# The last half sequence of a recurrence and its experts, taken as two parts of 256 tokens

## The chip, the cores and the metric

The kernel runs on one core of a Trainium2 chip. The core has five engines that work side by side, each with its own queue of instructions in a fixed order: TensorE (PE) for matmuls, VectorE (DVE), ScalarE (ACT), GpSimd (POOL), and SyncE (SP), which here issues most of the DMA transfers. They wait for each other through semaphores. The metric is device time of one launch in microseconds. The profile is one launch recorded by the hardware profiler.

## The reference: what is computed

Four layers, each with an attention-like part and a feed-forward part, act on 4 sequences of 1024 tokens with 128 features. The change touches the last layer only. It has a selective state-space recurrence, and then eight experts with gates:

```
x   = rms_norm(resid) * norm_w
xs  = silu(causal_conv4(x @ in_w.T) + conv_b)            # 256 channels
d   = softplus(xs @ wd1.T @ wd2.T + wd2_b)
h_t = exp(d_t * A) * h_{t-1} + (d_t * xs_t) * B_t        # 16 states a channel, over time
y   = (h . C + xs * W_D) * silu(x @ skip_w.T) @ out_w.T
x   = layernorm(resid + (resid + y))
gate = probs * keep          # softmax router, most probable experts up to a sum of 0.8
x   = layernorm(x + sum_e gate_e * (relu(x @ W1_e + b1_e) @ W2_e + b2_e))
```

All eight experts are computed for every token, and the gates weight their results. The recurrence runs along time, so a later piece of a sequence needs the last state of the piece before it (16 states for each of 256 channels), and the convolution needs the last three tokens.

## The kernel before, in words

The last layer takes the tokens in eight half sequences of 512. Each goes through these steps, written as Python generators that yield between small groups of instructions:

- l3_prepare: normalisation, input projection (matmul pxe), convolution on DVE (xc), silu (xs), the projections pdb, and softplus on ACT and DVE (dl, ud). The rows of B and C go out to DRAM by an SP DMA (rows).
- l3_scan: for each of 16 states n, two SP DMAs broadcast row n of B and of C over the partitions (bn, cn, four buffers each). POOL multiplies db = ud * bn, ACT computes da = exp(dl * A) into PSUM, DVE runs the scan (L1828), POOL multiplies hc = db * cn. From the second sequence on every second hc is added to the one before by an accumulating DMA that POOL issues (L1843), and PE sums what is left over the states with an identity matmul (pys).
- l3_sum and l3_finish: the skip gate (psk), the output projection (po), layer normalisation, transposition of the result (pt), and the router (prl, then about 15 short DVE instructions) that ends in the gates gt.
- l3_ffn_head: transposes the gates (pgt), ACT copies them (gT), a matmul adds the experts' second biases (pb), and DVE starts the accumulator h_acc.
- l3_ffn: for each expert four matmuls ph of 512 columns, relu on ACT (hh), sixteen matmuls py, and four DVE instructions that add gate times result to h_acc. At the end layer normalisation and the output DMA (L183). An expert's weights, 512 KB, come by an SP DMA into one of three wh buffers (l3_weights), asked for two experts ahead.

The function l3 lays these over each other. While the scan of one half runs, each of its 16 states also advances the finish of the half before, the preparation of the half after, and three or four steps of the experts (work), which belong to the half two back. A half is given to the experts a few states after its router (the age in todo). After the last scan the finish of the last half runs beside the experts of the last but one, then the experts of the last half follow. Once everything is handed over ("all"), the next change from one half's experts to another's also closes the PSUM banks of the scan and opens eight banks for the experts.

The generators only set the order in which instructions are written down. The framework then orders them on each engine by its own estimate of when each becomes ready, and each engine runs its list strictly in that order. So an instruction that waits holds up everything behind it on its engine: a pys that waits for hc holds up the experts' matmuls, and a bn DMA that waits for a buffer holds up the wh DMA behind it on SP.

Of the kernel before, what the change touches and what calls it, by code (L numbers as in the profile page):

```python
# [10 lines left out]
F32 = mybir.dt.float32  # L11
# [7 lines left out]
P = 128  # L19
# [39 lines left out]
class Net:  # L59
# [1513 lines left out]
    def l3(self, moe, fp):  # L1573
# [5 lines left out]
        halves = [dict(b=b, h=h) for b in range(B) for h in range(2)]  # L1579
        for i, u in enumerate(halves):  # L1580
            u["prev"] = halves[i - 1] if u["h"] else None
        halves[0] = dict(self.c3["first"], **{k: halves[0][k] for k in ("prev",)})
        for i, u in enumerate(halves[1:], 1):
            u["prev"] = halves[i - 1] if u["h"] else None
        work = self.l3_experts(fp)
        end = iter(())
        for i, u in enumerate(halves):
            nxt = iter(())
            if i + 1 < len(halves):
                if halves[i + 1]["h"] == 0:  # L1590
                    while "done" not in self.m2["st"][halves[i + 1]["b"]]:
                        next(moe)
                nxt = self.l3_prepare(halves[i + 1])
# [54 lines left out]
    def l3_weights(self, i, wp):  # L1648
        if i < 2 * B * NE:
# [18 lines left out]
    def l3_early(self, pool):  # L1668
# [19 lines left out]
        u = dict(b=0, h=0, at=at, ff=self.bank("pj"))  # L1688
# [3 lines left out]
    def l3_prepare(self, u):  # L1692

        nc, c3, b, h = self.nc, self.c3, u["b"], u["h"]
        at, ff, dp = u.get("at", self.l3_at), u.get("ff", self.bank("ff")), c3["dp"]
        wdb = c3["we"][:, :, 0:ND]

        sq = at("sq3", [P, 4, D])
        ms = self.sm.tile([P, 4], F32, name="ms3")
        for k in range(4):  # L1700
            nc.scalar.activation(
                sq[:, k, :], self.xN[b][:, 4 * h + k, :], AF.Square, accum_out=ms[:, k : k + 1]
            )
# [3 lines left out]
        for k in range(4):  # L1707
            nc.scalar.activation(
                sq[:, k, :], self.xN[b][:, 4 * h + k, :], AF.Copy, scale=ms[:, k : k + 1]
            )  # L1710
        yield
        pt = ff([P, 4, P], "pt")
        for k in range(4):
            self.tr(pt[:, k, :], sq[:, k, :])
        xnT = at("xnT", [P, 512])
# [6 lines left out]
        tail = at("tail", [P, 2, K1]) if h == 0 else u["prev"]["tail"]  # L1722
        u["tail"] = tail
        xs = at("xs3", [P, 2, 512])
        for ec in range(2):
            p = ff([P, 512], "pxe")
            self.mm(p, c3["wskip"][:, 1, ec * P : (ec + 1) * P], xnT)
            xc = at("xc", [P, 512])
# [3 lines left out]
            o = K1 if h else 0  # L1732
            nc.vector.tensor_scalar(xc[:, o:], p[:, o:], w[K1], bias, ALU.mult, ALU.add)
            if h:
# [3 lines left out]
            for d in range(1, KCONV):  # L1738
                nc.vector.scalar_tensor_tensor(
                    xc[:, d:], p[:, 0 : 512 - d], w[K1 - d], xc[:, d:], ALU.mult, ALU.add  # L1740
                )
            if h == 0:
                nc.vector.tensor_scalar(
                    tail[:, ec, :], p[:, 512 - K1 :], w[0], bias, ALU.mult, ALU.add
                )
                for d in range(K1 - 1, 0, -1):
                    nc.vector.scalar_tensor_tensor(
                        tail[:, ec, 0:d], p[:, 512 - d :], w[K1 - d], tail[:, ec, 0:d],
# [8 lines left out]
        db = at("db1", [ND, 512])  # L1757
        rows = dp.tile([2 * NST, 512], F32, name="rows")
        p = ff([ND, 512], "pdb")
# [6 lines left out]
        dl, ud = at("dl", [P, 2, 512]), at("ud", [P, 2, 512])  # L1766
        for g in ((0,), (1,)) if "at" in u else ((0, 1),):
            us, v = at("sp_u", [P, len(g), 512]), at("sp_w", [P, len(g), 512])
            p2 = []
            for k, ec in enumerate(g):  # L1770
                p2.append(ff([P, 512], f"pd{ec}"))
# [21 lines left out]
    def l3_scan(self, u):  # L1793


        nc, c3, b, h = self.nc, self.c3, u["b"], u["h"]
        sp, wp, aneg = c3["sp"], c3["wp"], c3["aneg"]
        wout = c3["we"][:, :, ND:]
        xnT, xs, dl, ud, rows = (u[k] for k in ("xnT", "xs", "dl", "ud", "rows"))
        carry = wp.tile([P, 2, NST], F32, name="carry") if h == 0 else u["prev"]["carry"]  # L1800
# [4 lines left out]
        def add(n, hc):  # L1805
            if not py:
                py.extend(self.psb(f"y{ec}", [P, 512], f"pys{ec}") for ec in range(2))
# [5 lines left out]
        for n in range(NST):  # L1813
            bc = []
            for i, nm in enumerate(("bn", "cn")):
                t = wp.tile([P, 1, 512], F32, name=nm, bufs=4)
                r = i * NST + n
                nc.sync.dma_start(
                    out=t[:, 0, :], in_=rows[r : r + 1, :].to_broadcast([P, 512])
                )  # L1820
                bc.append(t.to_broadcast([P, 2, 512]))
            db = wp.tile([P, 2, 512], F32, name="db", bufs=4)
            nc.gpsimd.tensor_mul(db, ud, bc[0])  # L1823
            for ec in range(2):
                j = ec * NST + n
                da = self.psb("da", [P, 512], "da")
# [5 lines left out]
                    carry[:, ec, n : n + 1] if h else 0.0,  # L1832
# [3 lines left out]
            if h == 0:  # L1836
                nc.scalar.copy(carry[:, :, n : n + 1], db[:, :, 511:512])
            hc = wp.tile([P, 2, 512], F32, name="hc", bufs=4)
# [25 lines left out]
    def l3_finish(self, u):  # L1864


        nc, c3, b, h = self.nc, self.c3, u["b"], u["h"]
# [4 lines left out]
        for ec in range(2):  # L1872
            p = ff([P, 512], "psk")
            self.mm(p, c3["wskip"][:, 0, ec * P : (ec + 1) * P], u["xnT"])

            t = sp.tile([P, 512], F32, name="th")
# [6 lines left out]
        po = ff([P, 4, D], "po")  # L1883
        for k in range(4):
# [9 lines left out]
        r = sp.tile([P, 4, D], F32, name="ss_r", tag="s2")  # L1894
        nc.vector.scalar_tensor_tensor(
            r, self.xN[b][:, 4 * h : 4 * h + 4, :], 2.0, po, ALU.mult, ALU.add
        )
        yield
        yield from self.norm_parts(wp, r, b, 4 * h, 4, ps=ff, act=True, slow=True)
        yield  # L1900
        n = NC // 2
        pr, g, rank, pj, cum = self.router(sp, b, c3["wr"], c3["br"], ps=ff, c0=4 * h, n=n)
# [12 lines left out]
    def l3_ffn_head(self, u, head, wp):  # L1915

        nc, c3, h = self.nc, self.c3, u["h"]
        ff = lambda s, n: self.psb("ff", s, n)
        acc = wp.tile([P, 4, D], F32, name="h_acc")
        head.append(acc)  # L1920
        pg = ff([NE, 4, P], "pgt")
        for c in range(4):
            self.tr(pg[:, c, :], u["gt"][:, c, :])
        gT = wp.tile([NE, 4, P], F32, name="gT", bufs=1)
        nc.scalar.copy(gT, pg)
        yield
        pb = ff([P, 4, D], "pb2")
        for c in range(4):
            self.mm(pb[:, c, :], gT[:, c, :], c3["b2"])
        nc.vector.tensor_add(acc, pb, self.xN[u["b"]][:, 4 * h : 4 * h + 4, :])  # L1930
# [247 lines left out]
```

## Time and profile before

| What | Value |
|---|---|
| Median of 3 runs | 2389.36 us (2387.49 to 2404.25) |
| The profiled execution | 2414.07 us, span 2412.3 us |
| Mean granted TensorE clock | 0.917 |
| Busy: PE, DVE, ACT, POOL | 2068.1, 1420.2, 1287.5, 863.0 us |
| First and last scan instruction of the layer on DVE | 1415.0, 2253.7 us |
| Experts, first and last ph | 1629.3, 2396.1 us |
| hc and db on POOL, 128 x 1024 elements | 2528 and 2638 ns each |
| Scan on DVE, 128 x 512, with carry | 1268 ns each |
| da on ACT, 128 x 512 | 689 ns each |

A row of instructions in the profile names the line, the engine, the operation, the result and the operands with their shapes, and how many there were. A matmul in 32-bit floats appears as two instructions. An idle time in brackets is what the engine waited before the instruction, with the engine or transfer that released it. All matmuls and transposes are issued from helper functions (L127, L131), so they are told apart by the names of their results: ph, py, pys and so on. Tiles keep their names in both kernels.

### The profile page before, as it was taken

What the parts mean: (1) busy time and instruction counts of PE and PEld (TensorE: products, weight loads), DVE (VectorE), ACT (ScalarE), POOL (GpSimd) and SP (SyncE); (2) the same over time, 40 slices, a digit from 0 to 9 for tenths busy, and PEclk for the clock granted to TensorE, in tenths of its full rate; (3) what the DMA queues carried; (4) which work ended last, traced back from release to release, by engine and by line L of the source; (5) the groups of instructions that cost most, each with busy time, mean ns of one, the idle gap of its engine ahead of it and who ended that gap; (6) DMA issues with size and microseconds to landing.
All of it is one profiled execution on the core that took longest, in us unless ns stands there. A gap on an engine that the chain in (4) does not pass through costs nothing.

```text
span 2412.3 us, 34775 instructions
## 1 busy us (share of the span) xinstructions
PE 2068.1 (86%) x12170; PEld 1454.9 (60%) x12170; DVE 1420.2 (59%) x3949; ACT 1287.5 (53%) x2679; POOL 863.0 (36%) x557
## 2 busy tenths in 40 slices
PE   6767979979899999999979965778797989899888
PEld 3455655544577787787767753346564656565566
DVE  6457733433455655655555676777777777687421
ACT  6543433332455555555556555565757766767443
POOL 5001220000000011001020148888877879589400
PEclk9657989989999999999999987789998989999899
DMA  3000110022000010021222155456764657476411
GB/s 101 0 18 20 32 31 9 9 86 71 1 1 1 1 34 21 11 81 43 65 64 82 35 181 176 140 176 178 193 198 135 181 154 207 139 205 176 114 57 49
DMA packets 138512, 209.84 MB, mean 87 GB/s; under 512 B 18597, under 2 KB 75936, under 8 KB 138080
## 3 DMA queue, kind: packets, MB, share of 16 engines
q1 hardware_dynamic: 126048, 172.82, 23.2%
q0 software_dynamic: 12288, 34.79, 6.9%
q8 instruction: 96, 1.57, 0.3%
q14 instruction: 80, 0.66, 0.1%
HBM read 159.24 MB, written 23.16 MB: 76 GB/s over the span
## 4 chain that ended last, share of the span: by engine, by line
PE 60%; DVE 18%; ACT 10%; issue 7%; DMA 2%; POOL 1%; another core or an unknown queue 1%; SPq 0%; ACTq 0%; POOLq 0%; DVEq 0%
PE ph L127 12%; PE py L127 8%; PE po L1118 4%; PE pqk L127 4%; PE po L127 4%; PE pt L131 4%; PE pa_m L127 3%; DVE db L1828 3%; PE pys L127 3%; PE po L1134 3%; PE kp_mo L127 3%; PE pv L127 2%; PE pr L127 2%; DVE a L1105 1%; PE kp_mo L131 1%
## 5 line engine op out<-in xcount | busy, mean ns | idle before, releaser
L1839 POOL TENSOR_TENSOR hc<-db,cn 128x1024 f32<-128x1024 f32 x128 | 317.1, 2528 | 88.8 <-PE pys L127 41.8
L1823 POOL TENSOR_TENSOR db<-ud,bn 128x1024 f32<-128x1024 f32 x112 | 287.1, 2638 | 29.3 <-DVE pmv L159 23.2
L127 PEld LDWEIGHTS py<-wh,hh 128*128 128x128 f32 x2048 | 253.7, 197 | 70.5 <-issue 40.9
L127 PE MATMUL ph<-xT,wh 128*128 128x512 f32 x512 | 265.3, 637 | 33.5 <-DVE h_acc L1967 13.4
L127 PE MATMUL py<-wh,hh 128*128 128x128 f32 x2048 | 259.8, 281 | 14.6 <-ACT hh L1951 9.5
L1951 ACT ACTIVATE hh<-ph,sb_cols 128x512 f32<-128x512 f32 x256 | 171.8, 682 | 158.6 <-PE ph L127 127.2
L1151 DVE SCALAR_TENSOR_TENSOR num<-po,sb_c_trig,nsin 128x130 f32<-128x130 f32 x256 | 89.2, 348 | 268.5 <-ACT nsin L1150 251.2
L1827 ACT ACTIVATE da<-dl,aneg 128x512 f32<-128x512 f32 x224 | 153.3, 689 | 66.7 <-DVE db L1828 63.2
L127 PE MATMUL pys<-hc,sb_c_ident 128*128 128x512 f32 x320 | 168.6, 655 | 15.6 <-POOL hc L1839 8.2
L1026 POOL MEMSET cv<- 128x16 f32 x32 | 4.1, 128 | 482.6 <-ACT cv L1043 365.5
L1828 DVE TENSOR_TENSOR_SCAN db<-da,carry,db 128x512 f32<-128x512 f32 x128 | 157.4, 1268 | 20.4 <-POOL db L1823 10.2
L127 PEld LDWEIGHTS ph<-xT,wh 128*128 128x128 f32 x512 | 93.9, 204 | 123.6 <-issue 56.5
L1150 ACT ACTIVATE nsin<-po,sb_c_trig 128x130 f32<-128x130 f32 x256 | 94.8, 370 | 131.7 <-PE po L1134 72.3
L1828 DVE TENSOR_TENSOR_SCAN db<-da,db 128x512 f32<-128x512 f32 x128 | 149.6, 1206 | 14.3 <-ACT da L1827 6.7
L127 PE MATMUL pqk<-xT,wE 128*128 128x256 f32 x512 | 138.9, 395 | 16.7 <-DVE cv L1036 13.7
L1967 DVE SCALAR_TENSOR_TENSOR h_acc<-py,gt,h_acc 128x128 f32<-128x128 f32 x256 | 72.1, 343 | 130.3 <-PE py L127 125.0
L1366 POOL DMA_INDIRECT xrows<-xN,di x64 | 62.4, 976 | 238.1 <-ACT kN L1070 230.6
L1118 PE MATMUL po<-cv,a 128*128 128x130 f32 x1024 | 138.7, 279 | 1.0 <-DVE num L1151 0.8
L1118 PEld LDWEIGHTS po<-cv,a 128*128 128x128 f32 x1024 | 126.8, 194 | 5.1 <-PE pqk L127 1.1
L1043 ACT ACTIVATE cv<-cv,sb_c_trig 128x520 f32<-128x520 f32 x128 | 86.5, 724 | 77.3 <-DVE cv L1036 68.2
L127 PEld LDWEIGHTS pys<-hc,sb_c_ident 128*128 128x128 f32 x320 | 63.3, 211 | 85.3 <-issue 60.4
L127 PEld LDWEIGHTS pqk<-xT,wE 128*128 128x128 f32 x512 | 88.5, 192 | 36.3 <-DVE cv L1036 18.1
(456 smaller groups left out, 4492.9 us busy)
## 6 DMA issues: line engine op xcount, KB each, us to landing
wx<-in_wF SPq DMA_DIRECT2D x92, 384.0 KB
bn<-rows SPq DMA_DIRECT2D x128, 256.0 KB
cn<-rows SPq DMA_DIRECT2D x128, 256.0 KB
wh<-in_wH SPq DMA_DIRECT2D x64, 512.0 KB
hc<-hc POOLq DMA_DIRECT2D x48, 512.0 KB
xrows<-zero SPq DMA_DIRECT2D x4, 1472.0 KB
xg<-xrows SPq DMA_DIRECT2D x20, 256.0 KB
yrows<-ys SPq DMA_DIRECT2D x20, 256.0 KB
```

Source lines behind the costliest of these rows:

```text
L127: return self.nc.tensor.matmul(out=out, lhsT=lhsT, rhs=rhs, start=start, stop=stop)
L131: self.nc.tensor.transpose(out, in_, self.ident[0:n, 0:n])
L1043: nc.scalar.activation(Q["v"][c][:, hs, i, :], v1[:, hs, :], AF.Copy, scale=c2["trig"][:, k, i : i + 1],)
L1118: self.nc.tensor.matmul(out=u["po"][:, i, c, :], lhsT=u["a"][:, i, c, :], rhs=Q["v"][c][:, 2 * hp + i, :, :].rearrange("p a d -> p (a d)") ...
L1134: self.nc.tensor.matmul(out=u["po"][:, i, c, :], lhsT=u["q"][h, s], rhs=Q["st"][h, hp, c, :], start=False, stop=True, skip_group_check=True,)
L1150: nc.scalar.activation(t, po[:, :, c, VW : 2 * VW], AF.Copy, scale=trig[:, k, 1:2])
L1151: nc.vector.scalar_tensor_tensor(num[:, c], po[:, :, c, 0:VW], trig[:, k, 0:1], t, ALU.mult, ALU.add)
L1823: nc.gpsimd.tensor_mul(db, ud, bc[0])
L1827: nc.scalar.activation(da, dl[:, ec, :], AF.Exp, scale=aneg[:, j : j + 1])
L1828: nc.vector.tensor_tensor_scan(db[:, ec, :], da, db[:, ec, :], carry[:, ec, n : n + 1] if h else 0.0, ALU.mult, ALU.add,)
L1839: nc.gpsimd.tensor_mul(hc, db, bc[1])
L1951: nc.scalar.activation(ht, ph, AF.Relu, bias=self.col("h_b1", i=e * NK + k))
```

## The change

The list of halves becomes a list of parts with a first chunk c0 and a length n in chunks of 128 tokens. The first seven parts are the half sequences as before (n = 4). The last half is replaced by two parts of n = 2. All shapes in the steps above follow n. The state (carry) and the last tokens for the convolution (tail) are kept whenever a part is not the last of its sequence, so they now pass from the first half of the last sequence to the first quarter part, and on to the second. The experts are run for nine parts instead of eight, so eight more loads of expert weights are issued. In an expert on 256 tokens the yield in the middle of py is left out.

```diff
-        halves = [dict(b=b, h=h) for b in range(B) for h in range(2)]
+        parts = [(b, h, 4) for b in range(B) for h in (0, 4)]
+        parts[-1:] = [(B - 1, 4, 2), (B - 1, 6, 2)]
+        halves = [dict(b=b, c0=c0, n=n, last=c0 + n == NC) for b, c0, n in parts]
         for i, u in enumerate(halves):
-            u["prev"] = halves[i - 1] if u["h"] else None
+            u["prev"] = halves[i - 1] if u["c0"] else None
...
     def l3_weights(self, i, wp):
-        if i < 2 * B * NE:
+        if i < self.c3["parts"] * NE:
...
     def l3_prepare(self, u):
+        L, first = n * P, c0 == 0
-        tail = at("tail", [P, 2, K1]) if h == 0 else u["prev"]["tail"]
-        u["tail"] = tail
-        xs = at("xs3", [P, 2, 512])
+        tail = None if first else u["prev"]["tail"]
+        u["tail"] = None if u["last"] else at("tail", [P, 2, K1])
+        xs = at("xs3", [P, 2, L])
...
     def l3_scan(self, u):
-                t = wp.tile([P, 1, 512], F32, name=nm, bufs=4)
+                t = wp.tile([P, 1, L], F32, name=nm, bufs=4)
...
-            db = wp.tile([P, 2, 512], F32, name="db", bufs=4)
+            db = wp.tile([P, 2, L], F32, name="db", bufs=4)
...
-                    carry[:, ec, n : n + 1] if h else 0.0,
+                    0.0 if first else carry[:, ec, n : n + 1],
...
-            if h == 0:
-                nc.scalar.copy(carry[:, :, n : n + 1], db[:, :, 511:512])
-            hc = wp.tile([P, 2, 512], F32, name="hc", bufs=4)
+            if not u["last"]:
+                nc.scalar.copy(carry[:, :, n : n + 1], db[:, :, L - 1 : L])
+            hc = wp.tile([P, 2, L], F32, name="hc", bufs=4)
...
     def l3_ffn(self, u, head, i0, wp, others):
-                ph = ff([P, 512], "ph")
+                ph = ff([P, n * P], "ph")
                 self.mm(ph, w[:, k * P : (k + 1) * P], x)
-                ht = wp.tile([P, 512], F32, name="hh", bufs=6)
+                ht = wp.tile([P, n * P], F32, name="hh", bufs=6)
...
-            py = ff([P, 4, D], "py")
-            for c in range(4):
+            py = ff([P, n, D], "py")
+            for c in range(n):
...
-                if c == 1:
+                if c == 1 and n > 2:
                     yield
```

## The prediction

> **What bounds the kernel now.** I number the half sequences 0 to 7. Half 7, the second half of the last sequence, is the one that becomes parts 7a and 7b. The views were read in this order: engine totals, then busy time by stage near the end, then TensorE's instructions at the stage boundaries, then who released each wait.
>
> Busy time by stage (columns: length, busy time of PE, its weight loads, DVE, ACT and POOL, then the granted clock and DMA):
>
> ```profile
> 2163.00:2184.00 21.00, 12.03 (x45) 6.43 (x43) 17.75 (x38) 13.44 (x19) 13.86 (x8) 0.84 0.64 166
> 2184.00:2256.00 72.00, 71.75 (x378) 48.98 (x376) 52.31 (x87) 47.95 (x76) 69.78 (x35) 1.00 0.66 182
> 2256.00:2275.00 19.00, 12.28 (x27) 6.17 (x28) 7.03 (x23) 4.44 (x9) 3.92 (x3) 0.64 0.39 88
> 2275.00:2344.00 69.00, 62.57 (x358) 46.15 (x356) 21.90 (x76) 29.22 (x44) 0.00 (x0) 0.97 0.20 61
> 2344.00:2404.00 60.00, 59.41 (x320) 41.99 (x320) 8.11 (x30) 22.88 (x36) 0.00 (x0) 0.95 0.17 49
> ```
>
> Row 2 is half 7's scan, with half 5's experts on PE beside it. PE is full at clock 1.00, and POOL nearly so. Rows 4 and 5 are the experts of halves 6 and 7 after the scan: PE again, and POOL has nothing left. Rows 1 and 3 are boundaries, where one scan ends and the next half's experts cannot start yet. PE loses time only there and at the hand-over at 2344.
>
> TensorE in order of time (start, length, what, then in brackets the idle before it and its releaser):
>
> ```profile
> 2250.21 3.82 PE L127 MATMUL py<-wh,hh 128*128 128x128 f32 x32
> 2253.86 1.88 PE L127 MATMUL pys<-hc,sb_c_ident 128*128 128x512 f32 x4
> 2261.48 1.02 PE L131 MATMUL pgt<-sb_c_ident,gt 128*8 128x128 f32 x4 [5.74 <-DVE gt L1910]
> 2263.73 2.07 PE L127 MATMUL pb<-sb_h_b,gT 8*128 8x128 f32 x8 [1.24 <-ACT gT L1925]
> 2265.74 5.49 PE L127 MATMUL ph<-xT,wh 128*128 128x512 f32 x6
> ...
> 2336.50 4.11 PE L127 MATMUL py<-wh,hh 128*128 128x128 f32 x32
> 2344.28 6.53 PE L127 MATMUL ph<-xT,wh 128*128 128x512 f32 x8 [3.67 <-DVE ln_nm L168]
> ...
> 2358.09 3.60 PE L127 MATMUL ph<-xT,wh 128*128 128x512 f32 x8
> 2361.53 3.73 PE L127 MATMUL py<-wh,hh 128*128 128x128 f32 x32
> ```
>
> At 2261 PE has waited 5.74 us for the router's gates (gt), then 1.24 us for their transpose's copy, and then runs at half clock: six ph take 5.49 us where six take 2.74 elsewhere. At 2344 it waits for the previous half's normalisation. The last two lines give the unit of work: an expert of 512 tokens is 3.44 us of ph and 3.57 us of py (start to start), 7.0 us.
>
> **The change part by part.**
>
> PE work: +0. The ph of 256 tokens stream half the columns. Matmuls of 512 columns start 0.43 us apart, those of 128 columns 0.11 us apart, so the time goes with the columns and 0.215 us is my estimate for 256. Twice as many at half length give 1.7 + 1.8 = 3.5 us per 256-token expert. The py, pys, pxe and psk keep their total columns. So the 221 us from 2183 to the last matmul still hold some 194 us of PE work: 24 experts of 512 tokens' worth (168) plus 26 of sums, projections and router. Splitting pulls nothing off PE. It lets half 6's experts and 7a's start inside the scan, but PE was not idle in the scan before. What can move is the time lost at boundaries, so I price those.
>
> New boundary, 7a to 7b. The nearest row is 2256:2275. From the first router instruction on DVE (2250.39) to gt (2261.43) took 11.0 us there. In the changed program's instruction order DVE also has the softplus chain of 7b in that stretch: ten instructions on 256 elements, 0.40 us each by the router's 128x256 rows, 4.0 us. It no longer has two scans there (2.45 us). So 12.6 us. Between router and gates PE has one expert's py (3.57) and the two pd (0.86). Idle 8.2, plus 1.2 for the copy. Then the half clock: pgt, pb and ph lost 0.4 + 0.9 + 2.75 = 4.1 us at 2261. The Trainium skill (TensorE: Matmul & The Clock Gate, "What's actually happening") says that an idle window of about 3.4 us halves the clock and some 3.4 us of sustained work restore it, which makes 1.7 us per gap. The row is dearer, because the sparse pgt and pb come first, so I take the row: 13.5 us (11.1 by the page). Ends: 6, if the gates come in time for PE, and 17, as the 2163:2184 row would give (12.5 us lost: 21 less 8.5 of work at full clock) with everything slower.
>
> Boundary 6 to 7a: half of the softplus work goes, ten DVE instructions at 0.67 falling to 0.40, -2.7 on the gates. Two of the pys that stood ahead of pgt now come behind it. Some of this falls on the half clock. -2 (0 to -4).
>
> Last boundary (now behind 7b): no scan is left in DVE's stretch (-2.45); the six 256-element router instructions become 128 (about -0.8); the one that took 2.12 us while POOL ran is nearer to the 0.42 it took at 2309, when POOL was idle (-1.8). Gates after 6 us, PE has 3.6 us to do, idle 2.4 instead of 5.74, and the half clock perhaps spared. -5 (0 to -8).
>
> Finish of the last part beside experts (L1873 to L1910): PE lost 1.67 + 1.25 and about 2 us of slow py around 2300. Two chunks instead of four shorten statistics and normalisation by 1.6. -1.5 (0 to -4).
>
> Hand-over 7a to 7b experts: the banks are still exchanged here, so ph still waits for the normalisation. 3.67 falls by 1.3 (h_acc, statistics), the slow ph (2.9) may go. -3 (0 to -5).
>
> End: from the last matmul to the end are 8.5 us. Two chunks save 0.5 of h_acc, 0.8 of statistics, 0.8 of xN and about 0.5 of the output's traffic. -2.6.
>
> Sums waiting for POOL: hc and db on half the elements are my estimate of 1.27 us (half of 2.53), 5.7 us for two states with their DMA issue. PE's order places the third sum 23 us after the gates, POOL and the accumulating DMA (6.1 us from 2167.86 to 2173.99) reach it at 27. The eighth is about even. Behind a late pys all experts' matmuls wait. +4 (0 to +8).
>
> Smaller instructions: the Trainium skill (VectorE: DVE Perf Modes, "The TRN2 errata") says that every instruction pays a fixed latency and asks for tiles of 512 elements or more. The rows agree on the size: 0.68 us for 512 elements, 0.42 for 256, so 0.16 is fixed. By the rule some 60 more DVE instructions cost 10 us. By the stage row DVE is busy 52 of 72 us while PE is full, so that is hidden and I take 0. If PE were not the bound it would show. ACT gets eight more table loads (1.28 us each); it is busy 48 of 72, so only one at the new boundary counts: +1.3.
>
> SP queue and loads: 64 row broadcasts of 128 KB replace 32 of 256 KB, and eight more expert weights (512 KB) are loaded. SP's issue is 0.33 to 0.4 us each, in stages of about 70 us. A bn waiting for a POOL buffer would hold back the wh behind it, but the order puts the wait about as late as the slot's release by PE. +0. The exception is the slow rival.
>
> Sum: 13.5 - 2 - 5 - 1.5 - 3 - 2.6 + 4 + 1.3 = +4.7 us on the profiled execution, 2412.3 us of span and 2414.07 in all. The runs' median, 2389.36, is 1% below it; I put the difference on the median: 2394.
>
> **The rivals.**
>
> *The new boundary is hidden (faster side).* At the boundary near 2075 pgt had no wait: other matmuls filled the time. If the gates come within PE's 4.4 us, 8.2 and 4.1 go: 2382, and with the other favourable ends about 2372. Against it: at two of three boundaries the rows show the wait, and in the changed order no sum is left to fill this one, since 7a's all stand earlier. 0.17.
>
> *Weight loads pace the 256-token experts (slower).* With three wh buffers, a slot freed by one expert's last py must be loaded before the ph three experts later: by the order, 3.9 us instead of 7.4. The load issued at 2357.84 moved its last bytes by 2360.9, 3.05 us, alone on the queues. That fits, with 0.7 us to spare for the release and semaphore. If landing takes more than 3.9 us it stretches each of some 14 experts; at 5.5 us, 14 x 1.6 = 22 us: 2416. It decides from 3.9 us on. Against it: no other traffic is left then, beyond 128 KB of output. 0.13.
>
> *As summed:* 2394. 0.70. That the change does not do what it says is excluded by the order: half 6's experts do stand beside 7b's sums, and only 7a's and 7b's follow.
>
> **How the numbers follow.** About 1%, 24 us, is what a measurement of this kernel can tell from no change. The likeliest case spans 2380 to 2408 by its ends. The range takes in most of the fast rival and the slow one up to its decision: 2376 to 2414. Faster by over 1% (below 2365) needs the hidden boundary and every other favourable end: 0.05. Slower (above 2413) is the slow rival, or all dear ends together: 0.14. The rest is 0.81.
>
> **What would show it.** Right: PE near full at clock 1.00 in both scans; a gap of 6 to 10 us ahead of pgt between 7a and 7b, with slow ph after it; POOL busy about 45 of 70 us in each scan; after 7b's scan some 65 to 70 us to the end instead of about 155; ph of 256 columns 0.215 us apart; no wait for wh. Wrong: gaps ahead of ph in the last 56 us released by DMA wh (slow rival); pgt without a gap (fast rival); long waits of pys for hc; or PE gaps inside the scans, which would mean that ACT or DVE queues, not PE, set the pace with shorter instructions.

## The result, and the profile after

The changed kernel takes 2409.9 us, the kernel before, run beside it, 2395.56 us. The ratio is 1.0066, with a 95% interval of 1.0049 to 1.0082: about 16 us slower. It lies in the range of the prediction and within 1% of no change, but the likeliest value was meant as +4.7 us, and the measured change is more than three times that.

I compare the two profiles over one stretch: from PE's first pgt of half 4's experts, which stand beside the scan of half 6, to the end of the span. Before that point both kernels run the same code. The stretch is 336.9 us before (2075.40 to 2412.3) and 354.7 us after (2060.69 to 2415.4), +17.8 us. That answers to the timed +16. The two spans differ by 3.1 us only, because the profiled execution of the kernel before reached that point some 15 us later. That is how far single profiles can differ: in ten profiles of versions that share the code up to there, the point comes between 2057 and 2075 us. The profiled execution of the changed kernel, 2417.18 us, is itself 7 us above the median of its runs.

How much of it is work? Matmuls follow each other every 0.43 us with 512 columns, 0.215 us with 256, 0.111 us with 128. Their counts times these give 276.7 us of PE work in the stretch before and 276.6 us after. So PE's work is the same, and its losses went from 60 to 78 us. The whole change is in the losses.

Busy time by stage of the changed kernel, cut where PE starts the experts of halves 4, 5 and 6 and of parts 7a and 7b (columns: the stage, its length, busy time of PE, its weight loads, DVE, ACT and POOL, then the granted clock, the DMA share and GB/s):

```profile
2060.00:2160.00 100.00, 83.03 (x406) 54.12 (x405) 75.12 (x157) 69.30 (x127) 81.28 (x40) 0.92 0.61 164
2160.00:2250.00 90.00, 80.52 (x418) 56.66 (x417) 52.23 (x133) 55.13 (x116) 47.20 (x42) 0.94 0.51 127
2250.00:2335.00 85.00, 72.44 (x383) 52.39 (x384) 39.65 (x104) 47.07 (x83) 46.16 (x40) 0.94 0.47 115
2335.00:2368.00 33.00, 29.11 (x167) 24.80 (x166) 10.56 (x42) 18.78 (x40) 0.00 (x0) 0.90 0.30 89
2368.00:2415.00 47.00, 39.26 (x250) 35.63 (x248) 9.14 (x35) 21.59 (x48) 0.00 (x0) 0.95 0.32 96
```

Rows 2 and 3 are the two short scans, each with a boundary at its start: POOL is busy for about half of each. Without the boundaries they read (from 2173 to 2244 and from 2262 to 2331, same columns):

```profile
2173.00:2244.00 71.00, 69.25 (x392) 51.50 (x391) 39.77 (x97) 40.91 (x86) 36.41 (x32) 1.00 0.52 130
2262.00:2331.00 69.00, 62.12 (x352) 46.53 (x352) 29.62 (x75) 35.79 (x63) 37.03 (x33) 1.00 0.50 119
```

So PE is still near full beside 7a, and no longer beside 7b. Rows 4 and 5 of the first table are what is left behind the last scan: 80 us, where the kernel before had 151 (2261.48 to 2412.3). The edit did shorten that part; it paid for it in the scans.

TensorE of the changed kernel in order of time (start, length, what, in brackets the idle time before it and its releaser):

```profile
2149.46 1.88 PE L127 MATMUL pys<-hc,sb_c_ident 128*128 128x512 f32 x4
2159.82 1.01 PE L131 MATMUL pgt<-sb_c_ident,gt 128*8 128x128 f32 x4 [8.48 <-DVE gt L1915]
2160.62 3.62 PE L127 MATMUL pys<-hc,sb_c_ident 128*128 128x512 f32 x4
...
2240.63 3.74 PE L127 MATMUL py<-wh,hh 128*128 128x128 f32 x32
2250.02 1.01 PE L131 MATMUL pgt<-sb_c_ident,gt 128*8 128x128 f32 x4 [5.66 <-DVE pmv L159]
2254.00 2.07 PE L127 MATMUL pb<-sb_h_b,gT 8*128 8x128 f32 x8 [2.96 <-ACT gT L1930]
2256.00 5.78 PE L127 MATMUL ph<-xT,wh 128*128 128x512 f32 x8
...
2282.53 1.13 PE L127 MATMUL pys<-hc,sb_c_ident 128*128 128x256 f32 x4 [3.77 <-DMA hc<-hc]
...
2328.03 0.51 PE L127 MATMUL prl<-sb_h_router,xT 128*128 128x8 f32 x4
2328.39 3.82 PE L127 MATMUL py<-wh,hh 128*128 128x128 f32 x32
2334.90 0.38 PE L131 MATMUL pgt<-sb_c_ident,gt 128*8 128x128 f32 x2 [2.69 <-DVE gt L1915]
...
2390.20 1.99 PE L127 MATMUL ph<-xT,wh 128*128 128x256 f32 x8
2392.03 1.95 PE L127 MATMUL py<-wh,hh 128*128 128x128 f32 x16
```

There are three boundaries with a wait for gates: 8.48 us ahead of pgt at 2159.82, 5.66 us at 2250.02 (the new one), and 2.69 us at 2334.90. In the kernel before, one boundary of the stretch waited for gates (5.74 us at 2261.48) and one for a sum (6.51 us at 2173.99, shown below). After each of the three, ph or pys run at half speed: eight ph take 5.78 us at 2256 where they take 3.4 elsewhere. The last two lines show the new unit of work: an expert of 256 tokens is 1.83 us of ph and about 1.8 of py.

PE's waits of the changed kernel from 2170 to 2416 (engine, tile and line that waited, for whom; us in total, times, longest):

```profile
PE pys L127 <- DMA hc<-hc: 7.8, 3, 3.8
PE pgt L131 <- DVE pmv L159: 5.7, 1, 5.7
PE pb L127 <- ACT gT L1930: 3.5, 2, 3.0
PE pgt L131 <- DVE gt L1915: 2.7, 1, 2.7
```

The largest total is not that of a gate but of sums waiting for POOL's accumulating DMA, three times inside the short scans. The longest single wait in this window is that for the gates of the new boundary, 5.7 us. (A wait named after pmv is the same wait for the gates: gt was DVE's work just beside it.) No wait for wh is among them.

POOL of the changed kernel where 7b's scan begins:

```profile
2249.47 4.92 POOL L1829 TENSOR_TENSOR db<-ud,bn 128x512 f32<-128x512 f32 x4 [31.90 <-DVE prl L1912]
```

POOL had finished 7a's products and stood idle for 31.90 us. What it waited for is 7b's ud, which DVE writes last at 2248.92, among the instructions of the router (prl, the name given, is DVE's work just beside it). The preparation of 7b is spread over the sixteen states of 7a in the order of PE and DVE, so POOL can't begin 7b before this stage ends.

### The profile page after: what moved, and what is told of

It reads as the page before. It is cut to its first block, busy times and chain, and to the rows that moved or that the text cites. A ratio compares the mean times of both kernels' runs of the same rounds, so it can differ in the third digit from the quotient of the medians.

```text
span 2415.4 us, 35387 instructions
## 1 busy us (share of the span) xinstructions
PE 2068.0 (86%) x12282; PEld 1477.7 (61%) x12282; DVE 1445.3 (60%) x4039; ACT 1315.5 (54%) x2788; POOL 874.9 (36%) x597
## 5 line engine op out<-in xcount | busy, mean ns | idle before, releaser
L1845 POOL TENSOR_TENSOR hc<-db,cn 128x1024 f32<-128x1024 f32 (+1 forms) x144 | 320.1, 2263 | 107.5 <-PE pys L127 40.1
L1829 POOL TENSOR_TENSOR db<-ud,bn 128x1024 f32<-128x1024 f32 (+1 forms) x128 | 292.1, 2353 | 57.9 <-DVE prl L1912 31.9
L127 PE MATMUL ph<-xT,wh 128*128 128x512 f32 (+1 forms) x576 | 271.3, 592 | 39.7 <-DVE h_acc L1972 15.0
L1956 ACT ACTIVATE hh<-ph,sb_cols 128x512 f32<-128x512 f32 (+1 forms) x288 | 178.6, 634 | 142.0 <-PE ph L127 131.8
L1833 ACT ACTIVATE da<-dl,aneg 128x512 f32<-128x512 f32 (+1 forms) x256 | 161.6, 635 | 81.3 <-DVE db L1834 80.7
L1834 DVE TENSOR_TENSOR_SCAN db<-da,carry,db 128x512 f32<-128x512 f32 (+1 forms) x160 | 163.3, 1055 | 37.2 <-ACT da L1833 18.8
L127 PE MATMUL pys<-hc,sb_c_ident 128*128 128x512 f32 (+1 forms) x352 | 168.2, 604 | 17.4 <-DMA hc<-hc 8.6
L127 PEld LDWEIGHTS ph<-xT,wh 128*128 128x128 f32 x576 | 107.0, 206 | 119.7 <-issue 44.2
```

The source lines that it names most:

```text
L127: return self.nc.tensor.matmul(out=out, lhsT=lhsT, rhs=rhs, start=start, stop=stop)
L1833: nc.scalar.activation(da, dl[:, ec, :], AF.Exp, scale=aneg[:, j : j + 1])
L1834: nc.vector.tensor_tensor_scan(db[:, ec, :], da, db[:, ec, :], 0.0 if first else carry[:, ec, n : n + 1], ALU.mult, ALU.add,)
L1845: nc.gpsimd.tensor_mul(hc, db, bc[1])
L1956: nc.scalar.activation(ht, ph, AF.Relu, bias=self.col("h_b1", i=e * NK + k))
```

## The experiments

The theory to be tested: PE's work bounds this stretch; what the split costs are waits at fixed places of PE's in-order queue, in scan, preparation and router; the experts' smaller size costs nothing by itself. The rivals: the short experts themselves (more weight loads, more small instructions) cost it; or the gates' latency at the new boundary is all of it. All times are compared with the kernel before on the same chip.

**Only the experts in two.** Scan and preparation of half 7 stay whole; only its finish and its experts are taken in two parts.

```diff
-        parts[-1:] = [(B - 1, 4, 2), (B - 1, 6, 2)]
...
+        two = [dict(b=B - 1, c0=c, n=2, last=c == 6) for c in (4, 6)]
+        for k, v in enumerate(two):
+            s = slice(256 * k, 256 * k + 256)
+            v.update(xnT=u["xnT"][:, s], xs=u["xs"][:, :, s])
+        end = chain(self.l3_sum(u), self.l3_finish(two[0]), self.l3_finish(two[1]))
```

> Half 7 is prepared and scanned whole, as before; only its finish and its experts run in two parts of 256 tokens, with the eight more weight loads. Theory: no boundary is added, so no price; the end is 2.6 us shorter and one more hand-over costs 0 to 4 us: ratio 0.998 to 1.001. Rival (price in loads and short instructions of the experts): most of the 16 us are here, ratio 1.004 to 1.007.

Measured: 2393.73 us, ratio 0.9983 (0.9966 to 1.0000). TensorE of this version where the second part's experts begin:

```profile
2347.28 1.72 PE L127 MATMUL py<-wh,hh 128*128 128x128 f32 x14
2348.84 0.38 PE L131 MATMUL pgt<-sb_c_ident,gt 128*8 128x128 f32 x2
2349.05 0.39 PE L127 MATMUL py<-wh,hh 128*128 128x128 f32 x2
```

Its pgt stands among the first part's py, without a wait: the gates were ready. So eight more weight loads and the shorter instructions of finish and experts cost nothing, and the stretch is 4.3 us shorter than before (332.6). The gain of the edit is here, and its price lies in the scan and the preparation.

**The preparation in one piece.** Half 7 is prepared whole, and its two scans take slices of it.

```diff
...
+    def l3_prepare_two(self, us):
+        a = us[0]
+        W = dict(b=a["b"], c0=a["c0"], n=4, last=True, prev=a["prev"])
+        yield from self.l3_prepare(W)
+        for k, u in enumerate(us):
+            s = slice(256 * k, 256 * k + 256)
+            u.update(xnT=W["xnT"][:, s], rows=W["rows"][:, s])
+            u.update({m: W[m][:, :, s] for m in ("xs", "dl", "ud")})
```

> Half 7 is prepared in one piece of 512 tokens, as before; its scan, finish and experts run in two parts on slices of it. Theory: at the boundary from 7a to 7b the softplus chain (4 us on DVE) is gone from the stretch that ends in the gates, POOL can start 7b's products at once, and the sums of 7b wait less; the boundary shrinks from 12.6 to some 4 to 8 us and the waits of the second scan (6.5 us) go, against 2.7 us more at the boundary before: ratio about 1.002 to 1.004. Rival (price in loads and short instructions): nothing changes, 1.0066. If it is the gates alone, not softplus, that are late: boundary still 10 us or more, ratio about 1.005.

Measured: 2403.43 us, ratio 1.0030 (1.0019 to 1.0042), as the theory had it. TensorE of this version at the boundary of 7a and 7b:

```profile
2250.32 1.13 PE L127 MATMUL pys<-hc,sb_c_ident 128*128 128x256 f32 x4 [2.25 <-DMA hc<-hc]
2254.55 1.01 PE L131 MATMUL pgt<-sb_c_ident,gt 128*8 128x128 f32 x4 [3.10 <-DVE gt L1929]
2256.22 2.07 PE L127 MATMUL pb<-sb_h_b,gT 8*128 8x128 f32 x8 [0.66 <-ACT gT L1944]
```

From the first router instruction on DVE to gt, in the changed kernel and in this version:

```profile
2239.94 0.20 DVE L1213 TENSOR_TENSOR prl<-prl,sb_h_br 128x32 f32<-128x32 f32 x1 [3.17 <-PE prl L127]
2249.69 0.19 DVE L1915 TENSOR_TENSOR gt<-rt_p,prl 128x32 f32<-128x32 f32 x1
...
2242.61 0.20 DVE L1213 TENSOR_TENSOR prl<-prl,sb_h_br 128x32 f32<-128x32 f32 x1
2254.32 0.17 DVE L1929 TENSOR_TENSOR gt<-rt_p,prl 128x32 f32<-128x32 f32 x1
```

The boundary loses 8.4 us instead of 12.6, but not as the theory had it: without the softplus of 7b the gates take 11.9 us and not less than the 9.9 of the changed kernel, since scans stand in its place on DVE. The wait ahead of pgt is shorter because two sums of 7a now stand between router and gates on PE. And gT waits 0.66 us instead of 2.96: in the changed kernel ACT first does 7b's first da, and it loads tables for 1.28 us at 2249.75 and again at 2251.93. The waits for hc fall from 8.4 to 3.4 us, none of them in 7b's scan: POOL goes from 7a to 7b without a wait of over 3 us. The boundary of 6 and 7a is again as in the kernel before (12.7 us lost instead of 15.0). So the second preparation makes up about half of the loss; how this divides over these places was not tested one by one.

**Half 6 split instead of half 7.**

```diff
-        parts[-1:] = [(B - 1, 4, 2), (B - 1, 6, 2)]
+        parts[-2:-1] = [(B - 1, 0, 2), (B - 1, 2, 2)]
```

> Half 6, the first half of the last sequence, is split into two parts of 256 tokens in place of half 7; half 7 stays whole. Theory (each added part costs TensorE one boundary, about 12 to 13 us, and some 8 us of sums that wait for POOL; only the end of the kernel gets a part of it back, about 11 us, when it is the last part that is short): the price is paid here and nothing comes back, so about 25 us over the kernel before, ratio 1.008 to 1.012. Rival (the price lies in the eight more weight loads and the shorter instructions of the experts, wherever they stand): the same as the change, 1.0066, about 16 us.

Measured: 2448.6 us, ratio 1.0219 (1.0194 to 1.0245). Neither had that. It has as many weight loads and short experts as the changed kernel and is some 37 us dearer, so these alone can't be the price. Busy time by stage of this version, from the start of 6a's experts (columns as above), and PE at the end of the first stage:

```profile
2236.00:2302.00 66.00, 43.53 (x226) 33.19 (x227) 43.95 (x89) 43.19 (x79) 52.26 (x25) 0.81 0.68 191
2302.00:2363.00 61.00, 48.70 (x204) 32.86 (x203) 30.97 (x59) 25.21 (x48) 28.98 (x15) 0.81 0.36 93
```

```profile
2301.83 0.59 PE L131 MATMUL pgt<-sb_c_ident,gt 128*8 128x128 f32 x2 [13.34 <-DVE gt L1915]
```

The scan of half 7 runs through both stages, from 2246.03 to 2331.54 on DVE, and keeps POOL at work for some 80 us. It stands beside experts of 256 tokens only, so PE has 34 to 37 us of work in stages of 61 to 66 us and waits 13.34 us for the next gates. In the changed kernel short scans stand beside long experts, and the short experts come after all scans. So this trace says that what a cut costs depends on which experts stand beside which scan, not on the number of boundaries alone.

**The router earlier.** In the changed kernel, the finish advances two steps per state in the 256-token scans.

```diff
-                next(end, None)
+                for k in range(2 if u["n"] < 4 else 1):
+                    next(end, None)
```

> The changed kernel, with the finish of the part before advanced twice instead of once for each state during the two scans of 256 tokens, so that half 6's router stands about a dozen states earlier in every engine's order. Theory (the new boundary is PE waiting for the gates): the gap ahead of pgt between 7a and 7b goes, with the half clock behind it, 8 to 12 us: ratio 1.001 to 1.004. Rival (PE would wait there anyway, for POOL's sums or for the softplus chain): the gap moves to another releaser, ratio 1.006 to 1.007.

Measured: 2413.01 us, ratio 1.0079 (1.0054 to 1.0104). The theory's number is excluded; the rival's lies in the interval. TensorE of this version at the boundary of 7a and 7b:

```profile
2238.31 3.74 PE L127 MATMUL py<-wh,hh 128*128 128x128 f32 x32
2241.89 0.60 PE L131 MATMUL pgt<-sb_c_ident,gt 128*8 128x128 f32 x4
2243.68 1.15 PE L127 MATMUL pb<-sb_h_b,gT 8*128 8x128 f32 x8 [1.19 <-ACT gT L1931]
...
2254.68 0.80 PE L127 MATMUL py<-wh,hh 128*128 128x128 f32 x2 [2.88 <-ACT hh L1957]
```

The 5.66 us ahead of pgt are gone, as meant. But PE then waits for ACT: hh comes late behind 7b's first steps, and the boundary still loses 9.4 us. The wait for gates at the end of 7a's finish is 3.7 us instead of 2.69, and one of 4.3 us stands at the end of 7b's, where none was.

**The sums later.** The pys of the short scans stand four states behind their products instead of two; the hc of two states share a buffer.

```diff
+        lag = 4 if L < 512 else 2
...
-                sums.append((n, hc0, n + 2))
+                sums.append((n, hc0, n + lag))
```

> The changed kernel, with one edit: in the two 256-token scans the matmuls pys that sum the states are put four states behind their products instead of two (the hc of two states share one buffer, so that the memory stays the same). Theory: the 8.4 us in which PE waits for hc inside these scans (1.61 + 3.94 + 2.88) come from the accumulating DMA being late against PE's in-order queue, and PE is the bound there; so they go: 5 to 8 us less, ratio to the kernel before 1.003 to 1.0045 instead of 1.0066, and no pys with a wait for hc over 1 us. Rival: with the sums later, more of them stand around the router's boundary or are found late there too, and the time only changes place: 1.006 or more.

Measured: 2412.1 us, ratio 1.0061 (1.0043 to 1.0079), not to be told from the changed kernel. No pys waits for hc any more, as the theory had it, but the time is nearer to the rival's. TensorE of this version at the end of the last scan, then ACT at the same place:

```profile
2320.24 3.89 PE L127 MATMUL py<-wh,hh 128*128 128x128 f32 x32
2323.97 0.51 PE L127 MATMUL prl<-sb_h_router,xT 128*128 128x8 f32 x4
2333.34 0.59 PE L131 MATMUL pgt<-sb_c_ident,gt 128*8 128x128 f32 x2 [8.85 <-DVE gt L1921]
```

```profile
2326.78 1.28 ACT L1217 ACT_TABLE_LOAD   x1 [5.60 <-DVE prl L1216]
...
2328.26 1.28 ACT L164 ACT_TABLE_LOAD   x1
```

The later sums push the finish back in PE's order, so that no expert's py is left behind prl (in the changed kernel one is, from 2328.39). From prl to pgt PE is idle for all of the router: 8.85 us instead of 2.69. The chain that ended last passes there through two table loads of 1.28 us on ACT: the router's Exp meets the Sqrt of the outgoing half's normalisation. Here 6.2 of the 8.4 us are lost again. Where the rest went stays open: in its single profile the stretch is 7.1 us shorter than that of the changed kernel, in the timed runs 1.2 us, and the intervals of the two ratios leave room for some us of gain.

**Both of these.**

> The changed kernel with two edits at once: the sums four states behind in the 256-token scans, and the finish advanced two steps per state in them. With the later sums alone the waits of PE for hc went from 8.4 us to none, but the wait for the gates at the end of the last scan grew from 2.96 to 8.97 us. Theory: the first is repaid in the second only because the router of part 7a stands too near the end of PE's queue, so with the router earlier both go: 5 to 10 us less than the changed kernel, ratio 1.002 to 1.0045, and less than 4 us of waits for gates at the end of the last scan. Rival (the sums and ACT's and DVE's share of the finish take the places of the waits again): 1.0055 or more.

Measured: 2409.38 us, ratio 1.0053 (1.0034 to 1.0072). This lies between theory and rival, nearer to the rival, and the interval reaches both and takes in much of the changed kernel's. No sum waits for hc, and the wait at the end of the last scan is 3.7 us. But hh comes late three times (5.2 us in all), and the end of 7a's experts waits 4.7 us for 7b's gates. Each time the place changes and most of the loss stays.

**No accumulating DMA in the short scans.**

```diff
-            if n % 2 and b > 0:
+            if n % 2 and b > 0 and u["n"] == 4:
```

> The changed kernel, with one edit: in the 256-token scans no DMA adds the products of two states; PE sums all sixteen states itself. That is 8 more sums of 0.86 us in each part, 13.8 us of PE work in all, and no DMA stands between POOL's product and PE's sum. If PE's work is the bound throughout: plus 13.8, less the 8.4 us of waits for hc, ratio 1.008 to 1.010. If POOL's queue with the accumulating DMA sets the pace of these scans (the chain that ended last runs through them from 2258 to 2313 us of the changed kernel): the gates of the last scan come earlier by about the waits, and the ratio is 1.002 to 1.005.

Measured: 2424.89 us, ratio 1.0110 (1.0091 to 1.0130). That is just above the number of the reading in which PE's work is the bound, which the interval takes in; the reading with POOL's queue is excluded. Busy time from 2262 to 2337 in this version, most of 7b's stage:

```profile
2262.00:2337.00 75.00, 74.49 (x399) 55.56 (x398) 32.76 (x72) 38.81 (x73) 33.47 (x28) 0.97 0.31 90
```

PE is full, no sum waits for hc, and the 13.8 us of added sums come out as +10.5 us in the timed runs (1.0110 less 1.0066). Against the version with later sums, which has no waits for hc either, it is +11.8 us timed and +15.2 us in the profiled stretch. So in the short scans PE's work, and not POOL's queue, sets the time as soon as PE doesn't have to wait. At the end of the scan the gates come late here too, 8.9 us, as with the later sums. The chain that ended last in the changed kernel runs through POOL there and would have suggested otherwise:

```profile
2263.46 2.17 DMA hc<-hc
2265.63 0.84 POOL db L1829
2266.47 6.63 DMA hc<-hc
```

It shows who released whom, and not what would be won.

**Four parts of 128 tokens.**

> The changed kernel, with the last half taken in four parts of 128 tokens instead of two of 256. Theory (each part brings one more boundary that PE cannot fill, about 12 us, and the end gains only half as much as by the first cut, 4 to 6 us): 20 to 30 us above the changed kernel, ratio 1.014 to 1.020. Rival (what counts is only how much stands behind the last scan, which halves again): 1.000 to 1.006.

Measured: 2464.77 us, ratio 1.0276 (1.0258 to 1.0294): the theory's direction, but dearer than its number: 50 us above the changed kernel for two more cuts, and not 20 to 30. PE's waits in this version from 2170 on:

```profile
PE pgt L131 <- DVE gt L1915: 14.5, 4, 7.7
PE pys L127 <- DMA hc<-hc: 13.5, 7, 4.7
...
PE ph L127 <- DMA wh<-in_wH: 4.1, 7, 0.9
```

All kinds of waits grow together. As with half 6, scans now stand beside short experts: between 2328.87 and 2407.79 PE has 39 us of work in 79. That part was missing in the theory, which counted boundaries only.

**Only the experts in four.** As the first experiment, with four parts of 128 tokens.

> The kernel before with only the finish and the experts of the last half in four parts of 128 tokens (scan and preparation whole). It is asked when the loads of the experts' weights become the bound, the second rival of the forecast. PE needs 1.78 us for an expert of 128 tokens (half of 3.5 to 3.6), a load of 512 KB took 3.05 us alone. A slot's round is load, 0.7 us of release, and four groups of matmuls of 0.89 us, 7.3 us for three experts: 2.4 us for one. Theory: waits of ph for wh of some 0.6 us for each of about 28 experts, 16 to 20 us above the version with two parts (0.9983), ratio 1.004 to 1.008. Rival (loads overlap and are hidden): 0.997 to 1.000, no waits for wh.

Measured: 2419.88 us, ratio 1.0080 (1.0056 to 1.0104). PE's longest wait in this version from 2170 on:

```profile
PE ph L127 <- DMA wh<-in_wH: 8.0, 14, 1.5
```

Here the weights do pace the experts. The 16 experts between 2354.19 and 2394.43 take 2.5 us each, against 1.78 us of PE work; the theory had 2.4. Only 8.0 us carry the name of wh, so about a third of the 23 us by which this version is dearer than that with two parts. The rest are losses of 0.7 to 1.7 us between groups, which I have not taken apart one by one.

**Finish and preparation both twice per state, in every scan,** in the changed kernel, in the kernel before, and with only the experts in two:

```diff
-                next(end, None)
-                next(nxt, None)
+                for k in range(2):
+                    next(end, None)
+                for k in range(2):
+                    next(nxt, None)
```

> The changed kernel, with finish and preparation both advanced two steps per state in every scan. Theory (PE is the bound, and what the split costs are waits at fixed places): the wait ahead of pgt between 7a and 7b goes, as it did with the finish alone, but the work that fills PE's queue there is also moved, so that little is won: ratio 1.003 to 1.008. Rival (the gates are the whole cost of the new boundary, and preparation packed early leaves the later states free): 12 us less, 1.001 to 1.002.

> The kernel before, with finish and preparation both advanced two steps per state in every scan. If the waits for gates at the boundaries of the kernel before (6.8 us ahead of pgt at the boundary of halves 6 and 7) can be hidden by an earlier router, three or four boundaries give 10 to 20 us: ratio 0.991 to 0.996. If, as in the changed kernel with the finish alone advanced, the wait only turns into waits for hh and py with PE's queue in the same order: 0.998 to 1.004.

> The kernel before with only the finish and experts of the last half in two parts (scan and preparation whole), and with finish and preparation advanced two steps per state in every scan. The two edits touch different places, so theory: the ratio of the two-part experts (0.9983) times that of the earlier router alone in the kernel before, run beside it, within 0.0015. Rival: the earlier router changes the last half's end too, and the sum fails by more than that.

Measured: 2420.03 us, ratio 1.0100 (1.0081 to 1.0120), dearer than either expected; 2399.83 us, 1.0013 (0.9999 to 1.0027), in the range where waits only turn into others; and 2397.13 us, 1.0007 (0.9994 to 1.0020), against 0.9996 as the product of the two, within the 0.0015 that the theory allowed. In the kernel before so changed, the wait of 6.5 us for hc falls to 1.1 and that of 5.74 us for gates to 2.9, but waits of 3.6 us for gates and 4.4 us for gT stand where none or a shorter one was. Its stretch is 5.8 us shorter than that of the kernel before, while its timed ratio is not below 1: the scans ahead of the stretch seem to lose what it wins. That is read from single profiles and was not tested by itself, nor why the changed kernel loses more by the same edit.

No version beats the kernel before clearly. The one with only the experts in two is ahead by 4 us, with an interval that just reaches 1.

Where a version leaves the earlier scans alone, the profiled stretch less the 336.9 us of before agrees with the timed difference within 4 us, which is why I trust its parts to some us and no further:

| version | stretch, us | less before | timed, us |
|---|---|---|---|
| experts in two | 332.6 | -4.3 | -4.1 |
| preparation in one piece | 343.5 | +6.6 | +7.2 |
| later sums, earlier router | 347.0 | +10.1 | +12.7 |
| later sums | 347.5 | +10.6 | +14.6 |
| earlier router | 353.4 | +16.5 | +18.9 |
| the changed kernel | 354.7 | +17.8 | +15.8 |
| experts in four | 357.5 | +20.6 | +19.2 |
| no accumulating DMA | 362.7 | +25.8 | +26.4 |
| half 6 split | 386.0 | +49.1 | +52.5 |
| four parts | 400.1 | +63.2 | +66.2 |

## Why the prediction was right, and where it was not

The range held, and so did the picture in the main: PE bounds the stretch, its work stays, and what moves are losses, most of them at named places. The sum was short by 13 us on the profiled stretch (+4.7 for +17.8). As an absolute time, 2409.9 us lies above the likeliest case (2380 to 2408) and within the range only by the room that was left for the slow rival, which did not come; but 6 us of that are the kernel before, 2395.56 us here and 2389.36 in the runs that the prediction stood on.

Of the signs named for being right, three came: ph of 256 columns 0.215 us apart, no wait for wh, and POOL busy for some 46 us in each scan. PE was near full beside 7a only; the gap ahead of pgt was 5.66 us, just under 6; and behind 7b's scan it was 80 us to the end, not 65 to 70. One of the signs of being wrong came too, a long wait of pys for hc, 3.77 us in 7b's scan. Term by term (each good to some tenths):

| term of the sum | predicted, us | measured in the two profiles, us |
|---|---|---|
| PE work | 0 | -0.1 |
| new boundary, 7a to 7b (with one table load, +1.3) | +14.8 | 5.84 + 3.54 + 1.11 + 2.18 = +12.7 |
| boundary 6 to 7a | -2 | 12.6 to 15.0: +2.4 |
| last boundary | -5 | 11.5 to 6.2: -5.3 |
| finish of the last part | -1.5 | 5.1 to 4.1: -1.0 |
| hand-over | -3 | 6.5 to 4.25: -2.2 |
| end | -2.6 | 8.7 to 6.0: -2.7 |
| sums waiting for POOL | +4 | 1.61 + 3.94 + 2.88 = +8.4 |
| hh late beside 7a's preparation | not in the sum | 1.23 + 1.12 = +2.4 |
| the rest, small losses over the whole stretch | not in the sum | +3.2 |

**Right.** The gains at the last boundary and behind it came nearly as reckoned: 11.2 us for 12.1. The new boundary came out right as a sum, and partly by luck: PE waited 5.66 us for the gates and not 8.2, and 2.96 us for their copy and not 1.2. The gates came after 9.9 us instead of 12.6, mostly because the router's L1231, 2.12 us in the row that the estimate rested on, took 0.42; the copy waited behind 7b's first da and two table loads on ACT, of which the sum had one. For the clock behind these waits, the rule of the Trainium skill (TensorE: Matmul & The Clock Gate, "What's actually happening") gave an estimate of 1.7 us of lost clock for one gap (the second, 2.96 us, is shorter than its window of about 3.4) and the row of before 4.1; the changed kernel lost 0.6 + 1.11 + 2.18 = 3.9 us behind the two waits. The row was the better guide; whether it is because the sparse pgt and pb come first was not tested. The fixed part of DVE's short instructions stayed hidden: all finish and expert instructions of half 7 on halved tiles cost nothing in the version with only the experts in two.

**Wrong in sign: the boundary of 6 and 7a.** TensorE of the kernel before at this boundary:

```profile
2165.49 1.98 PE L127 MATMUL pys<-hc,sb_c_ident 128*128 128x512 f32 x4 [0.23 <-DMA hc<-hc]
2173.99 6.36 PE L127 MATMUL pys<-hc,sb_c_ident 128*128 128x512 f32 x8 [6.51 <-DMA hc<-hc]
2180.18 0.60 PE L131 MATMUL pgt<-sb_c_ident,gt 128*8 128x128 f32 x4
```

The wait ahead of pgt was one for hc and not for gates. The gates were there at 2176.74 (gt on DVE), while the last sums ended only at 2180. I had counted the router's shortening as a gain of this boundary. It did come: from the router's first DVE instruction to gt it is 14.6 us instead of 16.8. But the gates were not what ended last. With two of the three sums moved behind pgt, the sums' wait went and the wait for gates took its place, 8.48 us for 6.51. The half clock, which the sums had taken ahead of pgt (6.36 us for eight pys that take 3.4), now falls on a sum and on ph behind it. I had named the move of the sums and given it no price. The argument against the fast rival, that two of three boundaries wait for gates, rests on the same reading.

**Wrong in size: the sums waiting for POOL.** I reckoned 4 us for the third sum of 7b, and the row at 2282.53 shows 3.77. I had taken the eighth sum as even, and it waits 2.61 us (at 2313.28); that 7a's scan has such a wait too, 1.45 us (at 2222.16), was not considered. The products on POOL were near the estimate of 1.27 us: a median of 1.27 for hc and 1.57 for db. The accumulating DMA was longer than half of that on twice the data: for 256 KB a median of 4.4 us from issue to landing in 7a's scan and 5.6 in 7b's, against 6.7 us for seven of 512 KB in half 6's scan.

**Not foreseen: hh beside 7a's preparation,** 2.4 us. With the preparation in one piece a single wait of 0.4 us is left there, as in the kernel before, but one of 2.1 us comes up in 7a's scan. Why ACT is late was not tested.

**The rivals.** The new boundary was not hidden: 12.6 us. Where the router was moved so early that its wait did vanish, the boundary still lost 9.4 us, so even then that rival's 2382 us would not have come. The weight loads did not pace experts of 256 tokens: no wait for wh in the changed kernel. They do at 128 tokens, 2.5 us each, so the point from which that rival decides lies between 1.78 and 3.5 us of PE work per expert, below the size used here.

What the sum lacked most is shown by the experiments on single waits. The three ways to take away one of them (router earlier, sums later, both) change the time by no more than the measurement can tell from the changed kernel; in their traces the next late input stands a few us behind in PE's order. In all three a wait's length in the trace was more than its removal brought in the timed runs. Of the edits that keep the scan in two, only the one that does away with the second preparation brought its gain. Not tried was a version in which the sums of the short scans and the router are placed by hand.

## What to carry to other kernels

Where one in-order engine is the bound, cut into shorter parts only what comes last, behind everything that shares the engine: with the experts alone in two, the end's gain was kept and nothing was paid (4 us, at the edge of what the runs can tell); with the scan and its preparation cut too, another boundary and more late hand-overs turned this into a loss of 16 us. Where a preparation hides behind the part ahead of it, a cut shortens that cover: half of the loss went when the preparation stayed whole. Before you count a shorter wait as a gain, look at which input really ended last at that place, and at what other work covers the wait and where that goes in the new order. And look at what stands beside a shortened stage: a full-size scan beside half-size experts left the bound engine idle for almost half of the stage.

## What the runs showed of the hardware that was not expected

- The DMA that adds one 256 KB product to another from POOL's queue takes pieces of 2.2 to 6.6 us in the chain beside 7b's scan. Its median from issue to landing is 4.4 us in 7a's scan and 5.6 in 7b's, against 6.7 us for 512 KB in half 6's: half the bytes take clearly more than half the time.
- Halving the scan didn't halve POOL's stage: in the two short scans POOL is busy for 47 of 90 and 46 of 85 us, against 78 of 81 in the whole scan of the kernel before. Of the rest, 31.90 us are one wait for the next part's preparation; the others are for DVE's scan, for a DMA and for PE.
- Matmuls of 256 columns follow each other every 0.215 us at full clock, those of 512 and 128 every 0.43 and 0.111 us, so that the time goes with the columns down to 128; halving the tile cost TensorE nothing in itself.
